# Second matrix sum of a Fourier feed-forward layer for even and odd rows apart, with another order of vector and GpSimd work around it

## The chip, the cores and the metric

One Trainium2 chip; the kernel runs on one of its cores. The metric is device time in microseconds of one launch. The core's engines each run their own instruction stream in order and wait for one another by semaphores: TensorE (PE in the profile; PEld is its weight loads), VectorE (DVE), ScalarE (ACT), GpSimd (POOL) and SyncE (SP), which here only issues transfers. Matmuls write to PSUM, all else lives in SBUF. All data are float32.

## What is computed

A cross-attention block and a Fourier feed-forward layer, both with a residual:

```python
x = x + xattn(layernorm(x), ctx, mask, wq, bq, wk, bk, wv, bv, wo, bo)   # 16 heads of 32
x = x + ffn(layernorm(x), w_freq_real, w_freq_imag, bias)

# ffn:
w = complex(w_freq_real, w_freq_imag)          # 512 x 512
y = real(ifft(fft(x) @ w)) + bias
```

x is 2 x 2048 x 512, the context 2 x 128 x 512. In attention a score is multiplied by the mask, and a score of exactly 0 becomes -1e9 before the softmax over 128 keys.

The feed-forward layer is linear in its input, so it equals a product with one real 512 x 512 matrix. The kernel computes this matrix once (`m_ffn`), by two sums with tables of cosines and sines, and then multiplies every row by it.

## The kernel before

**Work and order.** The 4096 query rows are cut in 8 groups of 512, and each group in 4 tiles of 128. A tile is named (i, t), group and place in it; (1, 0), (1, 1) and (1, 2) are the fifth to seventh. The schedule is written out by hand: each engine runs its instructions in the order of the program's text, and the tile framework adds only the waits for data and for buffers.

For a tile, `begin` (L764) issues the scores on PE (`scores`, L316) into two PSUM banks, one for each half of the heads. For each half, `masked` (L343) multiplies by the mask on DVE (L345, reading PSUM), `maxima` (L349) marks zeros and finds minima on DVE (L352, L354, L355), `exponentials` (L357) does 8 exponentials with sums on ACT (L361), and `divided` (L370) a reciprocal on DVE (L373) and the division, normally on POOL (L374). Once both halves are divided, `transposed_weights` (L380) transposes the weights on PE (L400) and copies them out of PSUM on ACT (L391). `context` (L414) multiplies them with the values for a whole group. `Project` (o, L446) and `Ffn` (y, L489) are the products with `wo` and `m_ffn`; DVE adds the residual (L463, L528). `Queries` (q, L285) are the query products, `relative` (L234), `query_statistics` (L261), `query_norm` (L274) and `query_transposes` (L278) the layer norm in front of them; `relative` runs on POOL (L244) or ACT (L241, L242). `output_bias` (L438) adds a bias on POOL (L442). From tile (1, 2) on, `slot` (L769) holds the order of a tile; what it shall finish in the next tile is put on the list `carried`.

**Buffers.** PSUM has two buffers each for scores (`ps_sc`), transposes (`ps_tp`) and products (`ps_mm`). Work tiles rotate over a few buffers by tag: 2 for "parts" and "sums", 4 for "rel", 5 for the weights "w".

**The matrix.** `First` (L647) makes the first sum, four blocks of 128 rows, `half`. Its cosine and sine sums are each split by even and odd table rows, so that only the first quarter of the columns (QD = 128) is computed: eight matmuls of 127 to 129 columns for a block, two for each of four stretches of the bank (L672). `evict` copies the bank out on ACT (L685), `first` makes sums and differences of even and odd rows on POOL (L693, L695), and `second` sums and differences of the cosine and sine part on DVE (L706, L707), writing the second half of the columns backwards.

`Mirrored` (L727) makes the second sum, four blocks of `m_ffn`, m[0] to m[3]. It is split into cosines (even) and sines (odd) only: four matmuls of 257 or 255 columns for a block (L738). ACT evicts the even part with a bias `add` and the odd part (L748, L754), and POOL forms low = even + odd and, mirrored, high = even - odd (L755, L756). `add` comes from four rows of `half` through transfers (`load_first_rows`, L712) and one small transpose (`first_rows`, L719).

The blocks m[0] to m[2] stand in the hand-written order of tile (1, 0) (L985 to L1010), m[3] in that of tile (1, 1) (L1012 to L1032). The first y that needs them is that of `slot(1, 3)`.

Of the kernel before, what the change touches and what calls it, by code (L numbers as in the profile page):

```python
# [9 lines left out]
FP = mybir.dt.float32  # L10
# [12 lines left out]
def kernel(  # L23
# [261 lines left out]
    class Queries:  # L285


        def __init__(self, i, g, first=0, spare=False):
            self.i, self.g, self.first, self.spare = i, g, first, spare
# [13 lines left out]
        def evict(self, eng=nc.scalar):  # L303
            dst = qTs[self.i][:, self.g, self.first * P :]
            bias = bq[:, self.g : self.g + 1]
            if eng is nc.scalar:
                nc.scalar.activation(dst, self.ps, AF.Identity, bias=bias)
            else:
                eng.tensor_scalar(dst, self.ps, bias, None, ALU.add)
# [70 lines left out]
    def transposed_weights(i, t, first, end, eng=None, banks=None, later=None):  # L380

        if t == 0 and first == 0:
            pts[i] = [big_tile("pt", 6, f"pt_{i}_{g}") for g in range(NC)]
        ws = weights[i, t]

        def copy(g, ps):
            dst = pts[i][g][:, :, t * P : (t + 1) * P]
            if eng:
                eng.tensor_copy(dst, ps)
            else:  # L390
                nc.scalar.copy(dst, ps)  # L391

        for g in range(first, end):
            ps = (
                banks[g]
                if banks
                else ps_tp.tile([P, NR, P], FP, tag="tp", name=f"tpw_{i}_{t}_{g}")
            )
            for r in range(NR):
                nc.tensor.transpose(  # L400
                    ps[:, r, :], ws[r // 2].w[:, (r % 2) * NC + g, :], ident
                )
            if later is not None:
                later.append((copy, g, ps))
            elif not banks:
                copy(g, ps)
        if banks and later is None:
            for g in range(first, end):
                copy(g, banks[g])
# [234 lines left out]

    QD = HD // 2

    class First:  # L647


# [9 lines left out]
        def pe(self, between=()):  # L659
            ps = self.ps = ps_mm.tile([P, D], FP, tag="mm", name=self.name)  # L660
            at = 0


            for k, table, odd, n in (
                (0, cosines, 0, QD + 1),
                (0, cosines, 1, QD),
                (1, sines, 0, QD - 1),
                (1, sines, 1, QD),
            ):
                for b in range(2):  # L670
                    c = b * HC + odd
                    nc.tensor.matmul(  # L672
                        ps[:, at : at + n],
                        self.lhs[k](c),
                        table[:, c, :n],
                        start=(b == 0),
                        stop=(b == 1),
                    )
                at += n
                if at == D // 2 + 1:  # L680
                    call(between)
# [17 lines left out]
                    op,  # L699
                )  # L700

        def second(self):
            u = self.u
            cos, sin = u[:, :, 0, : QD - 1], u[:, :, 1, : QD - 1]
            d = self.dst.rearrange("p (a n) -> p a n", a=2)
            nc.vector.tensor_tensor(d[:, :, 1:QD], cos, sin, ALU.add)  # L706
            nc.vector.tensor_tensor(d[:, ::-1, HD - 1 : QD : -1], cos, sin, ALU.subtract)  # L707

    def half_of(g):
        return lambda i: half[:, i, g * P : (g + 1) * P]  # L710
# [13 lines left out]
        nc.scalar.copy(add, ps)  # L724
        return add

    class Mirrored:  # L727

        def __init__(self, name, lhs, dst):
            self.name, self.lhs, self.dst = name, lhs, dst

        def pe(self):
            ps = ps_mm.tile([P, D], FP, tag="mm", name=self.name)
            self.even, self.odd = ps[:, : HD + 1], ps[:, HD + 1 :]
            for i in range(NC):
                nc.tensor.matmul(  # L738
                    self.even if i < HC else self.odd,
                    self.lhs(i),  # L740
                    cosines[:, HC + i, :] if i < HC else sines[:, i, :],
                    start=(i % HC == 0),
                    stop=(i % HC == HC - 1),
                )

        def evict(self, add, eng=nc.gpsimd):
            low, high = self.dst[:, 1:HD], self.dst[:, D - 1 : HD : -1]
            nc.scalar.activation(  # L748
                self.dst[:, : HD + 1], self.even, AF.Identity, bias=add
            )  # L750
            odd = self.odd
            if eng is nc.gpsimd:
                odd = work.tile([P, HD - 1], FP, tag="odd", name=f"odd_{self.name}")
                nc.scalar.copy(odd, self.odd)  # L754
            eng.tensor_tensor(high, low, odd, ALU.subtract)  # L755
            eng.tensor_tensor(low, low, odd, ALU.add)  # L756

    carried = []

# [116 lines left out]


    h = [First(what, g) for what in range(2) for g in range(HC)]
    m = [Mirrored(f"m_{g}", half_of(g), m_ffn[:, g, :]) for g in range(NC)]
    rest = [Queries(0, g, 1, g >= HC) for g in range(NC)]  # L880
    q = [Queries(1, g) for g in range(NC)]
    values = [Values(b) for b in range(B)]
# [96 lines left out]
    w[1].exponentials()  # L979
    run(q[0])  # L980
    transposed_weights(0, 2, HC, NC)
    w[1].divided()

    load_mask(2)
    w = begin(1, 0)  # L985
    w[0].masked()
    m[0].pe()
    add = first_rows("add_m", rows_m)
    m[0].evict(add[:, 0:1])
    relative(3, 0, nc.scalar)  # L990
    w[0].maxima()
    relative(3, 1, nc.gpsimd)
    m[1].pe()
    m[1].evict(add[:, 1:2])
    relative(3, 2, nc.gpsimd)
    transposed_weights(0, 3, 0, HC)
    relative(3, 3, nc.scalar)
    w[0].exponentials()
    w[1].masked()
    w[1].maxima()  # L1000
    w[0].divided()
    m[2].pe()
    m[2].evict(add[:, 2:3])
    transposed_weights(0, 3, HC, NC)
    w[1].exponentials()
    query_statistics(3, 0, 2)
    q[1].pe()
    q[1].evict(nc.vector)
    w[1].divided()
    query_statistics(3, 2, TG)  # L1010

    w = begin(1, 1)  # L1012
    w[0].masked()
    context(0, 0, NC, nc.scalar, True)
    m[3].pe()
    m[3].evict(add[:, 3:4])
    w[0].maxima()
    q[2].pe()
    w[0].exponentials()
# [9 lines left out]
    query_norm(3, 0)  # L1029
    query_norm(3, 1)  # L1030
    w[0].divided()
    carried.append(lambda half=w[1]: half.divided(nc.vector))  # L1032


    for i in range(1, last - 1):
        p, pp, n, nn = i - 1, i - 2, i + 1, i + 2
        q = [Queries(n, g) for g in range(NC)]
        q_nn = Queries(nn, 0)
        o = [Project(p, t) for t in range(TG)]
        f_p = Ffn(p, 0)  # L1040
        if i > 1:
            load_rows(nn)
            load_mask(n)
            load_residual(p)
            f_pp = [Ffn(pp, t) for t in range(TG)]
            slot(
                i,
                0,
                [f_pp[1], f_pp[2], q[1]],
                turned=(p, TG - 1),  # L1050
                early=[(ffn_transposes, pp, 2)],
                pool=[(relative, nn, t, nc.gpsimd) for t in range(TG)],
                on_b=[(ffn_norm, pp, 3), (query_statistics, nn, 0, 2)],
                on_c=[(query_statistics, nn, 2, TG)],
            )
            slot(
                i,
                1,
                [q[2], q[3], f_pp[3]],
                turned=(i, 0),  # L1060
                early=[(context, p, 0, NC, nc.scalar, True), (ffn_transposes, pp, 3)],
                pool=[(output_bias, p)],
                on_b=[(query_norm, nn, 0), (query_norm, nn, 1)],
            )
        slot(
            i,
            2,
            o[:3],
            turned=(i, 1),
            early=[(query_transposes, nn, 0), (query_transposes, nn, 1)],  # L1070
            pool=[(output_bias, p, 0, HC)] if i == 1 else [],
            mid_a=[(output_bias, p, HC, TG)] if i == 1 else [],
            on_a=[(ffn_statistics, p, 0)],
            on_m=[(ffn_norm, p, 0), (query_norm, nn, 2), (query_norm, nn, 3)],
            on_c=[(ffn_statistics, p, 1)],
            end=[(ffn_transposes, p, 0)],
        )
        slot(
            i,
            3,  # L1080
            [o[3], f_p, q_nn],
            turned=(i, 2),
            early=[(query_transposes, nn, 2), (query_transposes, nn, 3)],
            on_a=[(ffn_statistics, p, 2)],
            on_b=[(ffn_norm, p, 1), (ffn_statistics, p, 3)],
            on_c=[(ffn_norm, p, 2)],
            end=[(ffn_transposes, p, 1)],
        )
# [201 lines left out]
```

## Time and profile before

| | us |
|---|---|
| median of 3 runs (lowest, highest) | 528.55 (528.09, 528.93) |
| profiled execution, time | 528.42 |
| profiled execution, span | 526.2 |

Busy time in stretches of the span, in us; the granted TensorE clock is 1.00 in all of them:

| stretch (us) | what | PE | DVE | ACT | POOL |
|---|---|---|---|---|---|
| 0 to 75.70 | set-up, first sum, group 0 | 73.93 | 59.33 | 47.94 | 47.93 |
| 75.70 to 125.13 | second sum, tiles (1, 0) to (1, 3), up to the first y | 48.57 | 41.98 | 37.27 | 35.00 |
| 125.13 to 442.30 | steady state | 317.06 | 273.69 | 222.39 | 203.63 |
| 442.30 to 526.20 | last tiles and their products | 80.40 | 54.83 | 35.62 | 43.36 |

How to read the profile: a float32 matmul shows as two records, so "x8" is four matmuls. Matmuls are pipelined and their ends are modelled, so the distance from one start to the next tells more of PE than a duration. A timeline line has start, duration, engine, line of the kernel, operation, names and shapes, a count, and, in brackets, the engine's idle time before it with what ended it. The chain of waits is followed back from the last instruction: at each step to what released it, or to the instruction before it on its engine.

### The profile page before, as it was taken

What the parts mean: (1) busy time and instruction counts of PE and PEld (TensorE: products, weight loads), DVE (VectorE), ACT (ScalarE), POOL (GpSimd) and SP (SyncE); (2) the same over time, 40 slices, a digit from 0 to 9 for tenths busy, and PEclk for the clock granted to TensorE, in tenths of its full rate; (3) what the DMA queues carried; (4) which work ended last, traced back from release to release, by engine and by line L of the source; (5) the groups of instructions that cost most, each with busy time, mean ns of one, the idle gap of its engine ahead of it and who ended that gap; (6) DMA issues with size and microseconds to landing.
All of it is one profiled execution on the core that took longest, in us unless ns stands there. A gap on an engine that the chain in (4) does not pass through costs nothing.

```text
span 526.2 us, 8813 instructions
## 1 busy us (share of the span) xinstructions
PE 520.0 (99%) x3028; PEld 295.1 (56%) x3028; DVE 429.8 (82%) x613; ACT 343.2 (65%) x1300; POOL 329.9 (63%) x272
## 2 busy tenths in 40 slices
PE   8999999999999999999999999999999999999997
PEld 7756676655545555555545555455545555455444
DVE  4789897799997988889887988889876899998351
ACT  3367789776666777766667777666686677666210
POOL 3779368566993569635993559634764466756450
PEclk9999999999999999999999999999999999999999
DMA  8962030000600042000600024000312001301002
GB/s 320 382 239 80 1 102 1 0 2 0 222 21 21 1 140 101 1 21 1 220 21 14 7 85 156 1 22 0 121 42 72 29 12 50 102 1 61 20 0 81
DMA packets 22892, 36.49 MB, mean 69 GB/s; under 512 B 2104, under 2 KB 7488, under 8 KB 22848
## 3 DMA queue, kind: packets, MB, share of 16 engines
q1 hardware_dynamic: 22160, 34.75, 19.3%
q10 hardware_dynamic: 688, 1.18, 0.6%
q8 instruction: 24, 0.39, 0.3%
q14 instruction: 20, 0.16, 0.1%
HBM read 27.53 MB, written 8.39 MB: 68 GB/s over the span
## 4 chain that ended last, share of the span: by engine, by line
PE 84%; DVE 8%; ACT 6%; issue 1%; POOL 0%; ACTq 0%; POOLq 0%; DVEq 0%
PE y L210 18%; PE q L210 18%; PE o L210 16%; PE tpw L400 8%; PE sc L326 6%; ACT w L361 5%; PE c L426 4%; PE tp_a L194 3%; PE tp_f L194 3%; DVE w L352 2%; DVE nmax L354 2%; PE half L672 1%; PE k L572 1%; PE v L210 1%; DVE w L345 1%; ACT pt L391 1%
## 5 line engine op out<-in xcount | busy, mean ns | idle before, releaser
L361 ACT ACTIVATE w<-w,nmax 128x128 f32<-128x128 f32 x512 | 198.3, 395 | 18.3 <-DVE nmax L355 14.6
L374 POOL TENSOR_TENSOR w<-w,rden 128x1024 f32<-128x1024 f32 x61 | 116.1, 1908 | 73.6 <-DVE rden L373 57.0
L210 PE MATMUL o<-wo,cT 128*128 128x512 f32 x256 | 115.4, 594 | 0.1
L210 PE MATMUL y<-m_ffn,nT 128*128 128x512 f32 x248 | 112.5, 595 | 0.3 <-DVE nT L198 0.2
L210 PE MATMUL q<-xnT,wq 128*128 128x512 f32 (+1 forms) x256 | 111.6, 580 | 0.0
L391 ACT COPY pt<-tpw 128x512 f32<-128x512 f32 x120 | 64.0, 586 | 54.8 <-PE tpw L400 54.7
L361 ACT ACTIVATION_READ_ACCUMULATOR w<-w,nmax 128x1 f32 x512 | 99.3, 194 | 0.0
L352 DVE SCALAR_TENSOR_TENSOR w<-w 128x1024 f32<-128x1024 f32 x64 | 88.3, 1380 | 0.9
L345 DVE TENSOR_TENSOR w<-sc,mask 128x1024 f32<-128x1024 f32 x64 | 77.5, 1212 | 10.1 <-PE sc L326 9.4
L354 DVE TENSOR_REDUCE nmax<-w 128x8 f32<-128x1024 f32 x64 | 78.1, 1220 | 2.2
L400 PEld LDWEIGHTS tpw<-ident,w 128*128 128x128 f32 x496 | 57.7, 141 | 30.5 <-issue 28.4
L210 PEld LDWEIGHTS o<-wo,cT 128*128 128x128 f32 x256 | 46.2, 190 | 47.8 <-issue 46.2
L210 PEld LDWEIGHTS q<-xnT,wq 128*128 128x128 f32 x256 | 46.4, 190 | 44.6 <-issue 40.2
L210 PEld LDWEIGHTS y<-m_ffn,nT 128*128 128x128 f32 x248 | 44.5, 190 | 45.2 <-issue 43.5
L482 POOL TENSOR_TENSOR x<-x,bf 128x512 f32<-128x512 f32 x32 | 50.4, 1574 | 24.7 <-DVE norm_f L227 24.7
L400 PE MATMUL tpw<-ident,w 128*128 128x128 f32 x496 | 64.3, 273 | 0.0
L223 POOL TENSOR_SCALAR rstd_f<-mv_f 128x1 f32<-128x1 f32 x32 | 19.0, 594 | 61.1 <-DVE mv_f L220 61.1
L442 POOL TENSOR_TENSOR x<-x,bo 128x512 f32<-128x512 f32 x32 | 47.3, 1509 | 0.0
L373 DVE RECIPROCAL rden<-den 128x8 f32<-128x8 f32 x64 | 12.7, 199 | 41.6 <-ACT w L361 41.4
L326 PEld LDWEIGHTS sc<-kT,qT 32*128 32x128 f32 x1024 | 31.5, 186 | 14.2 <-issue 12.5
L244 POOL TENSOR_SCALAR rel<-rows 128x512 f32<-128x512 f32 x23 | 38.5, 1688 | 1.2 <-DMA rows<-in_x_dram 1.2
L196 ACT COPY nT<-tp_f 128x512 f32<-128x512 f32 x29 | 16.9, 581 | 33.7 <-PE tp_f L194 33.5
(92 smaller groups left out, 551.5 us busy)
## 6 DMA issues: line engine op xcount, KB each, us to landing
rows<-in_x_dram SPq DMA_DIRECT2D x32, 256.0 KB, 4.2
x<-in_x_dram SPq DMA_DIRECT2D x32, 256.0 KB, 5.2
out_dram<-x SPq DMA_DIRECT2D x31, 256.0 KB, 2.0
mask<-in_mask_Bx1xSxS_fk_dram SPq DMA_DIRECT2D x8, 256.0 KB, 4.6
wk<-in_L_xattn_wk_w_dram ACTq DMA_DIRECT2D x2, 512.0 KB, 6.5
wq<-in_L_xattn_wq_w_dram SPq DMA_DIRECT2D x1, 1024.0 KB, 7.0
wr<-n_L_ffn_w_freq_real_dram SPq DMA_DIRECT2D x2, 512.0 KB
wi<-n_L_ffn_w_freq_imag_dram SPq DMA_DIRECT2D x2, 512.0 KB, 8.9
```

The lines of the kernel that those rows point to most:

```text
L210: nc.tensor.matmul(ps, lhs(c), rhs(c), start=(c == 0), stop=(c == NC - 1))
L244: eng.tensor_scalar(d, xt, xt[:, 0:1], None, ALU.subtract)
L326: nc.tensor.matmul(sc[r // 2][:, r % 2, g, :], qTs[i][rows, g, t * P : (t + 1) * P], kT[rows, g, b * K : (b + 1) * K], start=True, stop=True,)
L345: nc.vector.tensor_tensor(self.w, self.sc.rearrange("p r g k -> p (r g) k"), self.mrow, ALU.mult)
L352: nc.vector.scalar_tensor_tensor(w, w, 0.0, w, ALU.is_equal, ALU.subtract)
L354: nc.vector.tensor_reduce(self.nmax, w, AX.X, ALU.min)
L361: nc.scalar.activation(w[:, h, :], w[:, h, :], AF.Exp, bias=self.nmax[:, h : h + 1], scale=-UNIT, accum_out=self.den[:, h : h + 1],)
L374: eng.tensor_tensor(w, w, rden.unsqueeze(2).to_broadcast([P, HH, K]), ALU.mult)
L391: nc.scalar.copy(dst, ps)
L400: nc.tensor.transpose(ps[:, r, :], ws[r // 2].w[:, (r % 2) * NC + g, :], ident)
L442: nc.gpsimd.tensor_tensor(xs[:, t, :], xs[:, t, :], bo, ALU.add)
L482: nc.gpsimd.tensor_tensor(xt, xt, bf, ALU.add)
```

## The change

The list of (table half, table, odd, columns) of the first sum becomes a common `products`. The second sum gets the form of the first: `Second` takes the place of `Mirrored`. A block is four matmuls of 127 to 129 columns, each into its own stretch of the bank and each complete in itself; ACT evicts the bank in two instructions (129 columns with the bias, the rest without) into a work tile; then `first` on POOL and `second`, on DVE for m[0] and m[1], on POOL for m[2] and m[3], as its new argument `eng` says.

The order of tiles (1, 0) to (1, 2) changes too. m[1] is issued just behind m[0], and q[1] ahead of m[2]. `relative(3, 0)` moves ahead of the tile, and `relative(3, 3)` goes from ACT to POOL. The second division of tile (1, 0) and half of the statistics move behind the scores and the first masking of tile (1, 1). The second division of tile (1, 1) goes from DVE to POOL, with the first `output_bias` of group 0 ahead of it.

```diff
+    products = (
+        (0, cosines, 0, QD + 1),
+        (0, cosines, 1, QD),
+        (1, sines, 0, QD - 1),
+        (1, sines, 1, QD),
+    )
...
-        def second(self):
+        def second(self, eng=nc.vector):
...
-            nc.vector.tensor_tensor(d[:, :, 1:QD], cos, sin, ALU.add)
-            nc.vector.tensor_tensor(d[:, ::-1, HD - 1 : QD : -1], cos, sin, ALU.subtract)
+            eng.tensor_tensor(d[:, :, 1:QD], cos, sin, ALU.add)
+            eng.tensor_tensor(d[:, ::-1, HD - 1 : QD : -1], cos, sin, ALU.subtract)
...
-    class Mirrored:
+    class Second(First):
+        def __init__(self, g):
+            self.name = f"m_{g}"
+            self.dst = m_ffn[:, g, :]
+            self.lhs = half_of(g)
         def pe(self):
+            ps = self.ps = ps_mm.tile([P, D], FP, tag="mm", name=self.name)
+            at = 0
+            for k, table, odd, n in products:
                 nc.tensor.matmul(
+                    ps[:, at : at + n],
+                    self.lhs(k * HC + odd),
+                    table[:, HC + odd, :n],
+                    start=True,
+                    stop=True,
                 )
+                at += n
+        def evict(self, add):
+            t = self.t = work.tile([P, D], FP, tag="parts", name=f"t_{self.name}")
+            n = QD + 1
+            nc.scalar.activation(t[:, :n], self.ps[:, :n], AF.Identity, bias=add)
+            nc.scalar.copy(t[:, n:], self.ps[:, n:])
...
     transposed_weights(0, 2, HC, NC)
+    relative(3, 0, nc.scalar)
     w[1].divided()
     load_mask(2)
     w = begin(1, 0)
     w[0].masked()
     m[0].pe()
+    m[1].pe()
     add = first_rows("add_m", rows_m)
     m[0].evict(add[:, 0:1])
-    relative(3, 0, nc.scalar)
     w[0].maxima()
     relative(3, 1, nc.gpsimd)
-    m[1].pe()
-    m[1].evict(add[:, 1:2])
+    m[0].first()
     relative(3, 2, nc.gpsimd)
     transposed_weights(0, 3, 0, HC)
-    relative(3, 3, nc.scalar)
+    m[1].evict(add[:, 1:2])
+    m[1].first()
+    q[1].pe()
     w[0].exponentials()
     w[1].masked()
     w[1].maxima()
+    q[1].evict(nc.vector)
+    m[2].pe()
     w[0].divided()
-    m[2].pe()
+    relative(3, 3, nc.gpsimd)
+    transposed_weights(0, 3, HC, NC)
+    m[0].second()
+    m[1].second()
     m[2].evict(add[:, 2:3])
-    transposed_weights(0, 3, HC, NC)
+    m[2].first()
     w[1].exponentials()
     query_statistics(3, 0, 2)
-    q[1].pe()
-    q[1].evict(nc.vector)
-    w[1].divided()
-    query_statistics(3, 2, TG)
-
+    old = w
     w = begin(1, 1)
     w[0].masked()
+    old[1].divided()
+    query_statistics(3, 2, TG)
     context(0, 0, NC, nc.scalar, True)
     m[3].pe()
     m[3].evict(add[:, 3:4])
+    m[2].second(nc.gpsimd)
+    m[3].first()
+    m[3].second(nc.gpsimd)
     w[0].maxima()
...
     w[0].divided()
-    carried.append(lambda half=w[1]: half.divided(nc.vector))
+    output_bias(0, 0, 1)
+    carried.append(w[1].divided)
...
-            pool=[(output_bias, p, 0, HC)] if i == 1 else [],
+            pool=[(output_bias, p, 1, HC)] if i == 1 else [],
```

## The prediction

> **What bounds the kernel now.** I read the page first, then the chain of waits, then the timelines of the four engines from 75 to 126 us, the stretch that the change touches. The page says which engine matters:
>
> ```profile
> PE 520.0 (99%) x3028; PEld 295.1 (56%) x3028; DVE 429.8 (82%) x613; ACT 343.2 (65%) x1300; POOL 329.9 (63%) x272
> ```
>
> PE is busy all the time (and its granted clock is 1.00 in every stretch that I asked for), so a PE microsecond taken away ought to be a microsecond won. The chain of waits, followed back from the end, contradicts this for just our stretch (start, length, what):
>
> ```profile
> 79.06 1.94 PE m L738 x8
> ...
> 81.02 0.48 ACT m_ffn L748
> ...
> 96.80 0.18 DVE nmax L355
> ...
> 119.64 0.48 ACT nT L196
> 120.12 0.04 issue
> 120.16 0.66 PE tp_a L194 x4
> ```
>
> From 81 to 120 us the chain runs through ACT and DVE (evictions, exponentials, maxima), and PE comes back on it at 120.16. PE was packed full too, but its only idle time there is 0.73 us before that transpose and about 0.3 after. So two chains run side by side, about 1 us apart. From 125 to 441 us PE's pieces follow one another without a gap: what the first product of the second matrix (y, 125.13 us) gains or loses, the end gains or loses. I therefore forecast the start of that y.
>
> **The saved PE work.** The second sum's matmuls and the cheaper form already used in the first sum:
>
> ```profile
> 67.46 1.10 PE L672 MATMUL half<-dft,wi 128*128 128x129 f32 x8
> ...
> 76.74 2.00 PE L738 MATMUL m<-dft,half 128*128 128x257 f32 x8
> ...
> 120.16 0.66 PE L194 MATMUL tp_a<-ident,rel 128*128 128x128 f32 x4 [0.73 <-ACT nT L196]
> ```
>
> The durations (second column) include the pipeline's tail; from start to start the chain gives 1.93 for eight old records (one m) and 0.94 for eight of 128 columns (67.46 to 68.41). The new m has eight such records: 4 x (1.93 - 0.94) = 3.96 us less PE. Had the weight loads (190 ns each) set the pace, an m would take 1.5 us, but the first sum's eight records already go at 0.94.
>
> **What it adds.** Per m: ACT still evicts 512 columns in two instructions (0.62 us before; a single 512-column eviction of the first sum took 0.58, so 0.58 to 0.65, and ACT has idle time for either). POOL had two of 0.73; now `first` has 0.67 + 0.20 + 0.67 + 0.20 by the first sum's rows (L693, L695), 1.60 from start to start. `second` is two more of 254 columns: on DVE for m0 and m1, 0.33 each, 4 x 0.33 = 1.32 us; on POOL for m2 and m3. No POOL row has exactly that form; L693 (0.67) and the mirrored L755 (0.73) bound it from both sides. I take both; these end 1.2 us before POOL is wanted, so nothing follows. Moved: `relative(3,0)` goes into ACT's idle time at 77.6 (ACT waits there until 79.09), `relative(3,3)` goes from ACT to POOL (1.55), the division of tile 6's second half from DVE (1.38) to POOL (1.87), and one bias addition (1.25) ahead of that division on POOL. The DMA orders do not change; the four rows for `add` still land just before 78.86, so the first eviction cannot start before 79.29.
>
> **The price that the sum of busy times hides.** DVE and POOL exclude one another for some instructions:
>
> ```profile
> 74.59 2.10 POOL L374 TENSOR_TENSOR w<-w,rden 128x1024 f32<-128x1024 f32 x1
> ```
>
> ```profile
> 74.51 0.42 DVE L706 TENSOR_TENSOR half<-u_half 128x254 f32<-128x254 f32 x1 [0.73 <-POOL u_half L693]
> 74.85 2.12 DVE L707 TENSOR_TENSOR half<-u_half 128x254 f32<-128x254 f32 x1
> ...
> 107.35 2.28 DVE L352 SCALAR_TENSOR_TENSOR w<-w 128x1024 f32<-128x1024 f32 x1
> ...
> 139.33 0.54 DVE L355 TENSOR_SCALAR nmax<-nmax 128x8 f32<-128x8 f32 x1
> ```
>
> L707 is the second half of `second`: 0.41 alone, 2.12 when POOL's division got in between. L352 (1.22 alone) and even the tiny L355 (0.17) stretch likewise beside POOL's additions, and POOL's instructions stretch when DVE was first (L223, 0.23, took 1.11 at 113.86). Reads of PSUM (L345, L463), the reduction L354 and the statistics L219 never stretch. So who asks first holds until done. The change puts four more such instructions on DVE and fourteen more on POOL (16 of `first` and 4 of `second` for the 8 of before, one `relative`, one division) in the same stretch.
>
> One POOL instruction is milder. Beside L244 (`relative`, 1.57 us, from 139.16) the L355 above got through 0.53 us after L244's start, well before L244's end, so I let L244 block for 0.53. The Trainium skill, "SBUF — State Buffer", section "Who interferes with whom", says otherwise: whichever of the two engines issues first keeps the shared ports for the whole instruction. By that page the sum would end 1.6 us later, near 531.9 (an estimate); I take the row.
>
> **The sum.** I laid the instructions of all four engines end to end in the new order, with these durations, each starting when its engine is free and its inputs are ready (0.04 us after DVE or ACT, 0.07 after POOL, 0.2 after PE), first come first served between DVE and POOL. The old order laid the same way puts PE's q at 94.62 (trace 94.34), the scores of tile 7 at 103.25 (103.05), its weight transposes at 108.71 (108.52), and y at 125.50 (125.13). So the method is 0.1 to 0.4 late.
>
> DVE, from the first maxima of tile 5 (81.58 in the trace) to the first of tile 6 (96.97), took 15.39 us, of which 1.19 and 2.26 idle. In the new order the idle 3.45 goes, since no division waits at the head of the queue any more; `second` adds 1.32; 0.73 is waiting for m1's `first`, which stands on POOL behind two `relative`s; and waits behind POOL add 0.30 (L352), 0.11, 0.20, 0.10 and 1.90 (`second`; the last one behind the division of tile 5, as at 74.85), 0.55 (L352 behind the next division) and 0.64 (L355 behind m3's `first`), together 3.80. 15.39 - 3.45 + 1.32 + 0.73 + 3.80 = 17.79: maxima at 99.4 instead of 97.0.
>
> ACT follows: exponentials of tile 6 at 99.4 and 105.0 instead of 97.0 and 102.6, ending at 108.2. The scores of tile 7 wait for ACT's copies out of the borrowed bank until 103.6. The second half's division: reciprocal at 108.2; POOL is in the bias addition until 108.5; DVE's L352, asking at 108.3, goes next until 109.7; the division runs to 111.58. PE's transposes of those weights start at 111.65 instead of 108.52. From there PE is packed: 15.5 us to y, where the trace has 16.6, because the idle 1.0 at 119 to 121 is gone. y at 127.16.
>
> As a check by PE alone: 3.96 saved, idle 7.0 in place of 1.0 to 1.1 (largest: 2.47 before those transposes, 2.28 before the scores, 0.73, 0.50, 0.34): +2.0. Against my own laying of the old order it is +1.65, against the trace +2.03; I take **+1.8**. The profiled execution has a span of 526.2 and a time of 528.42, 0.13 below the median of 528.55. 528.42 + 1.8 = 530.2, and from the median 530.35: forecast **530.3**, slower.
>
> **Rivals.** *The ports cost little: faster.* If DVE's and POOL's instructions miss each other, the 3.8 us and the waits at 108 vanish. Then the maxima of tile 6 come at 94.9, the last exponentials end at 103.5, POOL divides to 105.9, PE transposes at 106.1, 2.4 sooner than 108.52, and the idle 1.0 goes as well: y 3.5 sooner, 525.0. For it: PE's saving is real, and the two DVE idles are filled. Against it: L707's 2.12, in the same pairing. It wins over the old kernel when the waits that I count (3.8 + 0.7 on DVE, 1.1 at the division) come to less than some 3.5 us.
>
> *One turn won: no change.* The single dearest wait is m1's last instruction behind tile 5's division. If `second` gets its turns, it saves 1.4 us: y at 125.7, 529.0. Which of the two asks first hangs on less than 0.4 us, so this is near.
>
> *The saving does not show on PE.* Were an m 1.5 us instead of 0.94, PE would come 2.3 later to places where it waits anyway (4 us in all up to 104): still about 530.3. So the matmuls hardly decide.
>
> **Chances.** Forecast, 529.6 to 531.8: 0.55. Slower still: 0.05. No change, within 0.2% (527.5 to 529.6, about what a measurement of this kernel can tell): 0.17. Faster: 0.23. The range leaves out the slowest 0.05 and, of the faster case, what goes beyond 526.0 (some 0.1): 526.0 to 531.8. The forecast's own range is 529.6 to 531.8.
>
> **What would show it.** Right: m rows of about 0.94 us per eight; PE idle before the transposes of tile 6's weights (2 us or more) and the scores of tile 7; a `second` on DVE of about 2.3 us beside POOL's division; the first maxima of tile 6 after 98.5. Wrong: `second` at 0.42 four times, the maxima of tile 6 before 96, y before 124. If the y starts late but the end does not, a later stretch had slack that the chain does not show.

## The result and the profile after

The changed kernel took 528.66 us (median of 12 runs, 528.33 to 529.56), the kernel before 528.41 beside it (12 runs, 528.09 to 529.26). The ratio is 1.0004, with a 95% interval of 0.9995 to 1.0013: no change that can be measured. The forecast was 530.3. The profiled execution has a span of 526.7 us. (The profile of the experiment e5 is of a disturbed execution and is not read; e11 is the same kernel again.)

The page's busy line first:

```profile
PE 518.3 (98%) x3028; PEld 293.8 (56%) x3028; DVE 432.2 (82%) x616; ACT 342.2 (65%) x1298; POOL 339.2 (64%) x286
```

PE is down by only 1.7 us and POOL up by 9.3. PE's timeline, where the brackets give the idle time before the line and what ended it:

```profile
77.21 2.05 PE L740 MATMUL m<-dft,half 128*128 128x129 f32 x16
...
84.03 1.05 PE L740 MATMUL m<-dft,half 128*128 128x129 f32 x8
...
90.85 1.16 PE L740 MATMUL m<-dft,half 128*128 128x129 f32 x8 [0.22 <-ACT cT L434]
92.31 3.70 PE L210 MATMUL q<-xnT,wq 128*128 128x512 f32 x8 [0.29 <-ACT cT L434]
...
102.63 1.16 PE L326 MATMUL sc<-kT,qT 32*128 32x128 f32 x28 [1.02 <-ACT pt L391]
...
110.34 0.88 PE L400 MATMUL tpw<-ident,w 128*128 128x128 f32 x6 [1.54 <-POOL w L374]
```

The second sum is as cheap as forecast: where PE does not wait inside a block, its eight records take 0.89 to 0.99 us from start to start. But idle time has opened at exactly the two places that the prediction named, before the scores of tile 7 and before the weight transposes of tile 6, and two smaller ones beside the copies of `context`. The old idle 0.73 at 120 us is gone. DVE's timeline at `second` and at the second division of tile 6:

```profile
86.77 0.39 DVE L707 TENSOR_TENSOR m_ffn<-u_m 128x254 f32<-128x254 f32 x1
87.08 0.41 DVE L708 TENSOR_TENSOR m_ffn<-u_m 128x254 f32<-128x254 f32 x1
88.06 0.43 DVE L707 TENSOR_TENSOR m_ffn<-u_m 128x254 f32<-128x254 f32 x1 [0.57 <-POOL u_m L694]
88.40 2.12 DVE L708 TENSOR_TENSOR m_ffn<-u_m 128x254 f32<-128x254 f32 x1
...
107.23 0.20 DVE L373 RECIPROCAL rden<-den 128x8 f32<-128x8 f32 x1 [2.29 <-ACT w L361]
107.35 1.18 DVE L352 SCALAR_TENSOR_TENSOR w<-w 128x1024 f32<-128x1024 f32 x1
```

and POOL's at the same two places:

```profile
88.14 2.10 POOL L374 TENSOR_TENSOR w<-w,rden 128x1024 f32<-128x1024 f32 x1
...
105.86 1.27 POOL L442 TENSOR_TENSOR x<-x,bo 128x512 f32<-128x512 f32 x1
107.58 2.70 POOL L374 TENSOR_TENSOR w<-w,rden 128x1024 f32<-128x1024 f32 x1 [0.46 <-DVE rden L373]
```

The last instruction of m1's `second` (88.40) takes 2.12 us in place of 0.41, because POOL's division began 0.26 us before it. At 107.58 it is the other way round: DVE's L352 has begun at 107.35, and the division takes 2.70 instead of 1.90. The chain of waits (start, length, what) runs through both places:

```profile
88.06 0.43 DVE m_ffn L707
88.49 2.03 DVE m_ffn L708
...
97.77 0.65 DVE nmax L355
...
107.58 2.71 POOL w L374
110.29 0.05 issue
110.34 0.88 PE tpw L400 x6
...
125.83 3.44 PE y L210 x8
```

It leaves PE at 79.4 and comes back at 110.34; in the kernel before it came back at 120.16.

**How places are compared.** From the first y to the end of the span every kernel below (e5 apart) takes 401.1 to 401.5 us, so y decides, as the prediction has it. But the set-up ahead differs from one execution to another: the scores of tile 5 begin between 75.59 and 76.72. The table therefore counts from those scores (first start in the timeline). "Maxima" is the end of the first half's maxima of tile 6, "division" the end of tile 6's second division. The time is the median less that of the kernel before on the same chip.

| kernel | maxima | division | y | y against before | time against before | ratio (95%) |
|---|---|---|---|---|---|---|
| before | 21.34 | 31.79 | 49.32 | | | |
| changed | 22.30 | 34.17 | 49.56 | +0.24 | +0.25 | 1.0004 (0.9995 to 1.0013) |
| e1 | 20.61 | 31.36 | 48.89 | -0.43 | +0.11 | 1.0008 (0.9996 to 1.0020) |
| e2 | 22.91 | 34.79 | 50.17 | +0.85 | +1.07 | 1.0020 (1.0011 to 1.0029) |
| e3 | 19.75 | 33.64 | 51.99 | (clock, see e3) | -0.35 | 1.0002 (0.9987 to 1.0016) |
| e4 | 19.57 | 33.48 | 48.86 | -0.46 | +0.04 | 1.0003 (0.9995 to 1.0012) |
| e5 | | | | | -1.90 | 0.9970 (0.9957 to 0.9982) |
| e6 | 21.16 | 31.74 | 48.21 | -1.11 | -1.05 | 0.9984 (0.9975 to 0.9993) |
| e7 | 20.97 | 32.84 | 48.23 | -1.09 | -0.85 | one run |
| e8 | 22.30 | 33.33 | 50.87 | +1.55 | +2.52 | 1.0041 (1.0029 to 1.0053) |
| e9 | 21.79 | 33.67 | 49.05 | -0.27 | -0.64 | 0.9991 (0.9982 to 1.0000) |
| e10 | 21.16 | 33.04 | 48.43 | -0.89 | -0.58 | 0.9990 (0.9981 to 0.9999) |
| e11 | 20.08 | 31.96 | 47.34 | -1.98 | -2.04 | 0.9965 (0.9952 to 0.9977) |

One profiled execution stands beside a median here, so a few tenths between the two columns mean nothing.

**Where the saved time went.** Taken from start to start on PE between the scores of tile 5 and y, the four blocks of the second sum take 3.8 us, where packed old blocks (in e6, in which PE never idles there) take 7.4. That is about 3.5 us less work. What PE waits in the same stretch, every step against the same step in a packed stretch, grew from 1.1 to 4.7 us: 1.8 at the weight transposes of tile 6, 1.5 at the scores of tile 7, 0.8 beside the copies of `context`, and 0.6 in two small places. The gain turned into new waits, almost one for one. (The bracketed idle times are smaller, since the modelled end of a matmul covers part of a gap.)

### The profile page after: what moved, and what is told of

Read it like the earlier page. It is cut to its first block, busy times and chain, and to the rows that moved or that the text cites. A ratio compares the mean times of both kernels' runs of the same rounds, so it can differ in the third digit from the quotient of the medians.

```text
span 526.7 us, 8840 instructions
## 1 busy us (share of the span) xinstructions
PE 518.3 (98%) x3028; PEld 293.8 (56%) x3028; DVE 432.2 (82%) x616; ACT 342.2 (65%) x1298; POOL 339.2 (64%) x286
## 4 chain that ended last, share of the span: by engine, by line
PE 86%; DVE 7%; ACT 4%; POOL 2%; issue 1%; ACTq 0%; POOLq 0%; DVEq 0%
PE y L210 18%; PE q L210 18%; PE o L210 18%; PE tpw L400 9%; PE sc L326 6%; PE c L426 4%; ACT w L361 3%; PE tp_a L194 3%; PE tp_f L194 3%; DVE w L352 2%; PE half L673 1%; DVE nmax L354 1%; PE k L572 1%; PE v L210 1%; DVE w L345 1%; PE busy L544 1%
## 5 line engine op out<-in xcount | busy, mean ns | idle before, releaser
L374 POOL TENSOR_TENSOR w<-w,rden 128x1024 f32<-128x1024 f32 x62 | 119.0, 1923 | 69.0 <-DVE rden L373 53.5
L352 DVE SCALAR_TENSOR_TENSOR w<-w 128x1024 f32<-128x1024 f32 x64 | 88.4, 1381 | 0.8
L442 POOL TENSOR_TENSOR x<-x,bo 128x512 f32<-128x512 f32 x32 | 45.4, 1449 | 0.0
L244 POOL TENSOR_SCALAR rel<-rows 128x512 f32<-128x512 f32 x24 | 41.2, 1729 | 1.5 <-PE tp_a L194 1.5
L326 PE MATMUL sc<-kT,qT 32*128 32x128 f32 x1024 | 38.0, 283 | 1.0 <-ACT pt L391 1.0
```

The source lines that it names most:

```text
L244: eng.tensor_scalar(d, xt, xt[:, 0:1], None, ALU.subtract)
L326: nc.tensor.matmul(sc[r // 2][:, r % 2, g, :], qTs[i][rows, g, t * P : (t + 1) * P], kT[rows, g, b * K : (b + 1) * K], start=True, stop=True,)
L352: nc.vector.scalar_tensor_tensor(w, w, 0.0, w, ALU.is_equal, ALU.subtract)
L374: eng.tensor_tensor(w, w, rden.unsqueeze(2).to_broadcast([P, HH, K]), ALU.mult)
L442: nc.gpsimd.tensor_tensor(xs[:, t, :], xs[:, t, :], bo, ALU.add)
```

## The experiments

The theories, as the expectations name them. **A**, that of the prediction: PE's saved time is eaten by DVE's waits for GpSimd, and what queues behind them. **B**: the new order costs, and the form of the sum by itself gains 1 to 4 us. **C**: neither matters much; GpSimd's longer queue ahead of tile 6's second division decides. **D** was formed after e1 to e4: the order of tile 5 (two `relative`s ahead of `first`, q[1]'s eviction ahead of `second`) costs some 0.9 us, the rest of the new order gains, and y is set by the DVE and ACT chain and not by PE.

**e1: the new form in the old order.** `first` and `second` stand behind the evictions where the old blocks had their work. Against the kernel before, without the classes:

```diff
     m[0].evict(add[:, 0:1])
+    m[0].first()
     relative(3, 0, nc.scalar)
...
     m[1].evict(add[:, 1:2])
+    m[1].first()
     relative(3, 2, nc.gpsimd)
...
     transposed_weights(0, 3, HC, NC)
+    m[0].second()
+    m[1].second()
+    m[2].first()
...
     m[3].evict(add[:, 3:4])
+    m[2].second(nc.gpsimd)
+    m[3].first()
+    m[3].second(nc.gpsimd)
```

> The new form of the second sum (four quarter-column matmuls, first on GpSimd, second on DVE for blocks 0 and 1) in the order of the kernel before. Theory A (the saved PE time is real and is eaten by DVE's waits for GpSimd, and by what queues behind them): PE's rows for a block fall from 1.93 to about 0.95 us, yet the first maxima of tile 6 come at 98.5 to 99.5 us (97.0 before) and the time is 1.3 to 2.3 us above before. Theory B (the new order is what costs, the form by itself gains): 1 to 4 us below before. Rival C (GpSimd's longer queue alone): about 1 us above, with the maxima of tile 6 not later than 97.5.

No change in time. `second` on DVE, the division and the L352 behind it:

```profile
86.12 0.38 DVE L707 TENSOR_TENSOR m_ffn<-u_m 128x254 f32<-128x254 f32 x1
86.42 0.82 DVE L708 TENSOR_TENSOR m_ffn<-u_m 128x254 f32<-128x254 f32 x1
87.17 0.41 DVE L707 TENSOR_TENSOR m_ffn<-u_m 128x254 f32<-128x254 f32 x1
87.50 0.41 DVE L708 TENSOR_TENSOR m_ffn<-u_m 128x254 f32<-128x254 f32 x1
...
105.81 1.67 DVE L374 TENSOR_TENSOR w<-w,rden 128x1024 f32<-128x1024 f32 x1
107.41 2.28 DVE L352 SCALAR_TENSOR_TENSOR w<-w 128x1024 f32<-128x1024 f32 x1
```

With `first` early on POOL, `second` waits only 0.4 us for POOL, and the maxima of tile 6 come 0.7 sooner than before instead of later. So A's form in the expectation falls: `second` as such costs little; it cost much in the changed kernel because of where it stood. B's gain did not come either. DVE's division and L352 are held up by the four bias additions on POOL:

```profile
103.90 6.92 POOL L442 TENSOR_TENSOR x<-x,bo 128x512 f32<-128x512 f32 x4
```

**e2: the old form in the new order.** `Mirrored` as before, without `first` and `second`, in the changed order. Against the changed kernel:

```diff
-    class Second(First):
+    class Mirrored:
...
-    m[0].first()
...
-    m[1].first()
...
-    m[0].second()
-    m[1].second()
...
-    m[2].first()
...
-    m[2].second(nc.gpsimd)
-    m[3].first()
-    m[3].second(nc.gpsimd)
```

> The old form (257 and 255 columns, combined on GpSimd) in the new order. Theory A: no instruction of the second sum stands on DVE, but PE's 4 us are back, and the division of tile 6's second half on GpSimd still comes late: 0.5 to 1.5 us above before. Theory B (the order costs): 3 us or more above before. Rival C (GpSimd's queue decides): GpSimd has some 6 us less to do here than in the changed kernel, so the transposes of tile 6's weights come at 108.5 or sooner and the time is within 0.5 us of before.

1.07 us slower than before. The order costs without any `second` on DVE. The changed kernel is 0.8 us faster than this (+0.25 against +1.07), so the form does gain under the new order.

**e3 and e4: m0's and m1's `second` later.** e3 moves the two behind the first division of tile 6, with four buffers for the sums instead of two, so that they no longer meet the division of tile 5. e4 takes e3 and also the early bias addition away again.

```diff
-            u = self.u = work.tile([P, 2, 2, QD], FP, tag="sums", name=f"u_{self.name}")
+            u = self.u = work.tile([P, 2, 2, QD], FP, tag="sums", bufs=4, name=f"u_{self.name}")
...
-    m[0].second()
-    m[1].second()
...
     w[0].divided()
+    m[0].second()
+    m[1].second()
     output_bias(0, 0, 1)
```

and for e4 also

```diff
-    output_bias(0, 0, 1)
...
-            pool=[(output_bias, p, 1, HC)] if i == 1 else [],
+            pool=[(output_bias, p, 0, HC)] if i == 1 else [],
```

> The changed kernel with the two DVE seconds moved behind the norms of tile 6 (and four buffers for the sums, so that GpSimd does not wait for them). Theory A in its pure form: the maxima of tile 6 come 2.5 to 3.5 us sooner than in the changed kernel (about 95.5 instead of 98.4) and so does the end: 2.5 to 3 us below the changed kernel. Rival C (GpSimd's queue ahead of the division of tile 6's second half decides): the maxima come sooner just the same, but the division does not, and the time is 0.3 to 0.8 us below the changed kernel. Laying the rows end to end gives 0.6.

> As the run before, and the first bias addition (1.25 us on GpSimd) back behind the division of tile 6's second half. Theory A: as the run before, no further gain, since DVE's maxima are not touched. Rival C: another 1.0 to 1.3 us, some 1.8 us below the changed kernel and 1 to 1.5 us below before (0.2 to 0.3%).

The maxima of tile 6 come 2.5 to 2.7 us sooner, as they should if the turn behind the division cost 1.7 and the `second`s the rest. Yet by the ratios neither is apart from the changed kernel. e3 is 0.6 us below it by the medians, inside the intervals; that is what C and the laid rows had, and not the 2.5 to 3 of A. e4's further gain, which C needed, did not come. In e4 the late `second` met the next division, first on DVE

```profile
102.07 0.94 DVE L707 TENSOR_TENSOR m_ffn<-u_m 128x254 f32<-128x254 f32 x1
102.94 2.11 DVE L708 TENSOR_TENSOR m_ffn<-u_m 128x254 f32<-128x254 f32 x1
```

and on POOL

```profile
102.70 2.08 POOL L374 TENSOR_TENSOR w<-w,rden 128x1024 f32<-128x1024 f32 x1
```

So the same price, 2.11 for 0.41, is paid after all, only further down. It holds up DVE's next reciprocal until 106.11, and tile 6's second division ends only 0.7 us sooner (33.48 against 34.17). C is weakened: with the bias addition gone from POOL's queue nothing moved.

In e3's profiled execution PE's idle time before those transposes had a price of its own. The windows of 5 us, with the granted clock third from the right:

```profile
100.00:105.00 5.00, 5.00 (x48) 2.98 (x47) 5.00 (x8) 5.00 (x21) 5.00 (x7) 1.00 0.00 0
105.00:110.00 5.00, 2.41 (x8) 0.93 (x6) 4.93 (x6) 1.61 (x4) 4.75 (x3) 0.95 0.00 0
110.00:115.00 5.00, 4.76 (x11) 2.70 (x12) 4.90 (x7) 3.77 (x16) 5.00 (x5) 0.50 0.02 3
115.00:120.00 5.00, 5.00 (x18) 2.69 (x17) 4.36 (x7) 2.50 (x11) 3.15 (x4) 0.87 0.00 2
120.00:125.00 5.00, 5.00 (x51) 3.31 (x50) 2.55 (x5) 3.74 (x15) 3.28 (x4) 1.00 0.00 0
```

That execution took 531.74 us and is not the rule: the median of the 12 is 527.88.

**e5 and e11: the form in the old order of tile 5, with the rest of the new order.** e1, and `relative(3, 0)` early, the second division of tile 6 on POOL and the bias addition ahead of its first division.

```diff
     transposed_weights(0, 2, HC, NC)
+    relative(3, 0, nc.scalar)
     w[1].divided()
...
     m[0].first()
-    relative(3, 0, nc.scalar)
     w[0].maxima()
...
+    output_bias(0, 0, 1)
     w[0].divided()
-    carried.append(lambda half=w[1]: half.divided(nc.vector))
+    carried.append(w[1].divided)
...
-            pool=[(output_bias, p, 0, HC)] if i == 1 else [],
+            pool=[(output_bias, p, 1, HC)] if i == 1 else [],
```

> The new form in the order of the kernel before, with three pieces of the new order: relative(3,0) ahead of tile 5, the second division of tile 6 on GpSimd, one bias addition ahead of it (here also ahead of the first division, where GpSimd stood idle for 2 us). Theory D, formed from the first four runs (the new order of tile 5, with relatives and q[1]'s eviction ahead of first and second, costs about 0.9 us and the rest of the new order gains): y comes 1.2 to 2 us sooner than before, counted from the scores of tile 5 (49.3 before), and the time is 1.2 to 2 us below before (0.3%). Theory A (the saving goes to waits between DVE and GpSimd, whatever the order): no more than the 0.4 us of the form alone.

> The kernel of e5_form_part_order once more, for its profile: y 47.6 to 47.9 us after the scores of tile 5 (49.3 before), the maxima of tile 6 at 20.1 to 20.4 (21.3), tile 6's second division done by 32.2; 526.3 to 526.7 us.

526.40 and 526.31 us, 1.9 and 2.0 below before: this version beats both kernels, as D said. DVE in e11:

```profile
85.59 0.38 DVE L707 TENSOR_TENSOR m_ffn<-u_m 128x254 f32<-128x254 f32 x1
85.89 0.82 DVE L708 TENSOR_TENSOR m_ffn<-u_m 128x254 f32<-128x254 f32 x1
86.63 0.41 DVE L707 TENSOR_TENSOR m_ffn<-u_m 128x254 f32<-128x254 f32 x1
86.97 0.41 DVE L708 TENSOR_TENSOR m_ffn<-u_m 128x254 f32<-128x254 f32 x1
...
88.91 0.72 DVE L309 TENSOR_SCALAR qT<-q,bq 128x512 f32<-128x512 f32 x1
...
104.62 1.17 DVE L352 SCALAR_TENSOR_TENSOR w<-w 128x1024 f32<-128x1024 f32 x1
```

and POOL's last instruction ahead of the division of tile 5:

```profile
85.52 1.80 POOL L244 TENSOR_SCALAR rel<-rows 128x512 f32<-128x512 f32 x1
```

The last `second` has begun (86.97) before that division starts on POOL (87.29), and takes its own 0.41. The maxima of tile 6 come 2.22 us sooner than in the changed kernel, the division ends 2.21 sooner and y comes 2.22 sooner: one difference, made in tile 5, is carried unchanged to y. PE still waits for the division:

```profile
107.60 0.87 PE L400 MATMUL tpw<-ident,w 128*128 128x128 f32 x6 [1.21 <-POOL w L374]
```

**e6: only the bias additions of the kernel before earlier,** all four ahead of tile 6's first division.

```diff
+    output_bias(0)
     w[0].divided()
...
-            pool=[(output_bias, p, 0, HC)] if i == 1 else [],
-            mid_a=[(output_bias, p, HC, TG)] if i == 1 else [],
```

> The kernel before, old form and old order, only with the four bias additions of group 0 moved into GpSimd's idle time at 97 to 102 us, ahead of the first division of tile 6. Theory D and A both (what sets y is DVE's chain at tile 7, which stands behind GpSimd's additions for about 1.4 us, and not PE's matmuls): DVE's division falls from 1.38 to 1.2 us, the L352 behind it from 2.28 to 1.2, PE's idle 0.7 before the transpose goes, and y comes 0.7 to 1.0 us sooner, the time likewise. If PE's work sets y: no change.

1.05 us faster than before. DVE's division and L352, held up before, run at their own speed:

```profile
106.20 1.22 DVE L374 TENSOR_TENSOR w<-w,rden 128x1024 f32<-128x1024 f32 x1
107.34 1.22 DVE L352 SCALAR_TENSOR_TENSOR w<-w 128x1024 f32<-128x1024 f32 x1
```

since POOL is through with the additions:

```profile
96.73 5.95 POOL L442 TENSOR_TENSOR x<-x,bo 128x512 f32<-128x512 f32 x4
```

The 0.73 us of PE idle at 120 us was thus a consequence of POOL's additions beside DVE's division at 107, 13 us earlier. No PE idle is left in the stretch, from start to start; with the old form PE is then the bound.

**e10: the old form with e11's order.**

```diff
+    relative(3, 0, nc.scalar)
     w[1].divided()
...
     m[0].evict(add[:, 0:1])
-    relative(3, 0, nc.scalar)
...
+    output_bias(0, 0, 1)
     w[0].divided()
-    carried.append(lambda half=w[1]: half.divided(nc.vector))
+    carried.append(w[1].divided)
...
-            pool=[(output_bias, p, 0, HC)] if i == 1 else [],
+            pool=[(output_bias, p, 1, HC)] if i == 1 else [],
```

> The counterpart of the form in part of the new order, but with the old form: relative(3,0) early, tile 6's second division on GpSimd, one bias addition ahead. Theory D: PE's work counts only where DVE's and ACT's chain is out of the way; here PE and that chain are close to one another, y comes 0.3 to 0.5 us sooner than before, and the new form is worth 1.0 to 1.3 us against this kernel. If the form is worth nothing in any order: as fast as the form in part of the new order (526.4).

0.58 us faster than before, 1.46 slower than e11. So in this order the form is worth 1.5 us (1.1 by y) of the 3.5 that PE saves, and the three moves together 0.6. From start to start PE waits 0.2 us in e10 and 2.7 in e11: here the form gains until the DVE and ACT chain becomes the bound.

**e7: the turn at the division taken away.** The changed kernel, but the first division of tile 5 on POOL is a memset: half of that tile's weights are a constant, 0.01. The memset only writes.

```diff
+            if eng is None:
+                nc.gpsimd.memset(w, 0.01)
+                return
...
-    w[0].divided()
+    w[0].divided(None)
```

> The changed kernel with the division of tile 5's first half replaced by a GpSimd memset of the same 128 x 1024 weights (the first half of tile 5's weights is a constant here). It only writes. If the exclusion comes from GpSimd's reading: m1's second instruction on DVE, 2.12 us beside the division, takes 0.4 us although the memset runs beside it. If any GpSimd instruction holds DVE up: it lasts until the memset ends, 1 us or more.

DVE (this kernel has three lines more, so L711 is L708 of the others):

```profile
88.10 0.42 DVE L710 TENSOR_TENSOR m_ffn<-u_m 128x254 f32<-128x254 f32 x1 [0.57 <-POOL u_m L697]
88.44 0.42 DVE L711 TENSOR_TENSOR m_ffn<-u_m 128x254 f32<-128x254 f32 x1
```

POOL:

```profile
88.16 0.95 POOL L375 MEMSET w<- 128x1024 f32 x1
```

The last `second` ran wholly inside the memset and took 0.42 instead of 2.12. So DVE is not held up by POOL being busy as such; what the memset lacks is the reading. The maxima come 1.33 us sooner and so does y; 0.95 us of POOL's own time went too, so this bounds the price of that turn rather than giving it alone.

The Trainium skill, "SBUF — State Buffer", section "Who interferes with whom", says just this of a VectorE instruction with two SBUF inputs: it contends with a GpSimd instruction that reads SBUF, not with one that only writes. The 0.42 agrees.

**e8: tile 6's second division back on DVE,** in the changed kernel.

```diff
-    output_bias(0, 0, 1)
-    carried.append(w[1].divided)
+    carried.append(lambda half=w[1]: half.divided(nc.vector))
```

> The changed kernel with the second division of tile 6 back on DVE and the bias addition back behind it. Rival C (GpSimd's queue sets y): the transposes of tile 6's weights come 1 us or more sooner (34.2 us after the scores of tile 5 in the changed kernel) and y as well. Theory D: the transposes come 0.6 to 1.2 us sooner, but DVE's chain of tile 7 starts behind the division and behind the additions, so y comes 0.3 to 1.1 us later, and the time is 0.3 to 1.1 us above the changed kernel.

2.5 us slower than before, more than expected. The division does end sooner (33.33 against 34.17), but it meets POOL's additions, and the L352 behind it too:

```profile
107.03 1.96 DVE L374 TENSOR_TENSOR w<-w,rden 128x1024 f32<-128x1024 f32 x1
108.91 2.29 DVE L352 SCALAR_TENSOR_TENSOR w<-w 128x1024 f32<-128x1024 f32 x1
```

```profile
105.40 6.91 POOL L442 TENSOR_TENSOR x<-x,bo 128x512 f32<-128x512 f32 x4
```

As in the kernel before, DVE's lateness comes back on PE at 121 us (idle 0.92). So the move of the division to POOL, with the early bias addition that belongs to it, is a part of the change that gains; by C it should have been the part that costs. The median rose by 1.0 us more than y, but the profiled execution took 529.77 us, against a median of 530.82, and its span is 1.6 us longer than before, as its y says. No trace of an execution near the median is kept.

**e9: the changed kernel with m0's and m1's `first` ahead of the `relative`s on POOL.**

```diff
-    relative(3, 1, nc.gpsimd)
     m[0].first()
-    relative(3, 2, nc.gpsimd)
+    relative(3, 1, nc.gpsimd)
...
     m[1].first()
+    relative(3, 2, nc.gpsimd)
```

> The changed kernel with only GpSimd's order in tile 5 altered: m[0].first ahead of relative(3,1), and m[1].first ahead of relative(3,2). Theory D: m1's second on DVE no longer waits for GpSimd (idle 0.57 us before it in the changed kernel), the maxima of tile 6 come 0.7 to 1.0 us sooner (22.3 us after the scores of tile 5) and y and the time 0.6 to 1.0 us sooner than in the changed kernel. Theory A with any order alike: no change.

y comes 0.5 us sooner than in the changed kernel, and the time is 0.9 lower (-0.64 against +0.25). The wait of DVE for m1's `first` (0.57) is what this takes away; the maxima come 0.51 sooner, less than the 0.7 to 1.0 expected. The turn behind the division stays:

```profile
86.77 0.74 DVE L309 TENSOR_SCALAR qT<-q,bq 128x512 f32<-128x512 f32 x1
...
88.50 2.11 DVE L708 TENSOR_TENSOR m_ffn<-u_m 128x254 f32<-128x254 f32 x1
```

Here L309, q[1]'s eviction, stands ahead of the four `second`s; in e11 it stands behind them. Counted from the scores of tile 5, the division starts at 11.62 in e9 and 11.70 in e11, and the first `second` at 10.82 and 10.00. So the division comes at the same place, and most of the 0.8 us by which `second` is later in e9 is that eviction; no run moves it alone. The rest of the way to e11's maxima, 1.71 us, is the 1.70 that this turn costs.

## Why the prediction was right in its range and wrong in its number

**The range.** 528.66 lies in the stated range, 526.0 to 531.8, but only because the range takes in the rivals. The forecast's own part of it, 529.6 to 531.8, misses, and so does "slower"; what came is the case "no change", which had 0.17. That the range holds is its width, and not the sum.

**Right.** The form: m takes 0.89 to 0.99 per block, so the rival that PE does not show the saving is out. The place of the new waits on PE. The dearest turn: `second` behind the division of tile 5, 2.12. The order at tile 6's second half: DVE's L352 goes first, and the division waits. From the transposes to y 15.5 us (110.34 to 125.83), as laid. And that the idle at 119 to 121 us goes. Of its own signs, the maxima after 98.5 us and the idle of 2 us or more came out just short (98.41, in an execution whose set-up ran 0.5 us late; 1.8 from start to start).

**Wrong is a size: the waits behind POOL.** From the first maxima of tile 5 to those of tile 6 the sum had 17.79 us; it took 16.38. In the sum's terms (forecast, then measured):

| term | forecast | measured |
|---|---|---|
| L352, tile 5 | 0.30 | 0.13 |
| L355, tile 5 | none | 0.16 |
| `second` of m0, two | 0.11, 0.20 | 0, 0 |
| waiting for m1's `first` | 0.73 | 0.57 |
| `second` of m1, two | 0.10, 1.90 | 0, 1.71 |
| L352, tile 6 | 0.55 | 0.42 |
| L355, tile 6 | 0.64 | 0.47 |
| together | 4.53 | 3.46 |

Nearly every term is too large by 0.1 to 0.2. The two waits of m0's `second` did not come at all: DVE went first there. For the others, the laying let a waiting DVE instruction begin when POOL's had ended in the profile, and some hundredths later. The trace has it otherwise: the L708 that waited ended at 90.52, so with its own 0.41 it began at 90.11, while POOL's division shows until 90.24. The wait ends some 0.13 us before the profile's end of the POOL instruction. The row at 74.85 that the prediction shows had this already: 2.12 for 0.41 is a wait of 1.71, not 1.90. By the table, the four waits that came as forecast are 0.66 too large together, of which 4 x 0.13 = 0.52 is that end; three that did not come had 0.41; the wait for `first` is 0.16 too large, and L355 of tile 5, put at nothing, takes 0.16 back. The other 0.3 us are durations and latencies that each were some hundredths too long.

**And a turn that was not taken.** At tile 6's second half the sum had POOL in the bias addition until 108.5. That addition was over at 107.13, before the reciprocal at 107.23, so that the division waited only for DVE's L352, 0.8 us. It ended at 34.17 instead of 35.94 after tile 5's scores (111.58 less 75.64): 1.8 us less, of which 1.4 comes from the maxima. All of it is found again at y: 49.56 in place of 51.35 (127.16 less 75.64, and less 0.17, since the chain starts y that much later than the timeline).

**What that makes of the sum.** +2.03 was forecast for y against the trace, +0.24 was measured. The sum is a small difference of large terms, 3.96 saved against 6.0 more idle; the saving was 3.5 and the new waits 3.6. The saving was itself too large by 0.5, because the old blocks, one after the other in a packed stretch, take 1.74 to 1.94 and not 1.93 each.

**The rivals.** "One turn won" gave 529.0 and so stands nearest, but its mechanism did not happen: the turn was lost, as forecast, and the time stayed the same for another reason, the many small waits. What it says is still seen: where the turn is won without moving anything else (e7), y is 1.3 us sooner, near the 1.4 that the rival named, though e7 also takes 0.95 us off POOL. "The ports cost little: faster" needed waits of less than some 3.5 us, on DVE and at the division together; they were 3.46 and 0.8, so it missed its point by 0.8 us.

**What the prediction did not do** is part the form from the order. Against before, the form alone is worth nothing measurable (e1), the order alone costs 1.07 (e2). But the order is not one thing: early `relative(3, 0)`, the division on POOL and the early bias addition gain together (e10; for the last two e8, by its opposite), while the order of tile 5 loses the 2.2 us by which e11 is ahead at the maxima of tile 6: 0.5 by the `relative`s ahead of `first` (e9), and 1.7 because `second` comes so late that it meets the division. That q[1]'s eviction makes it so late is read from the traces of e9 and e11 and not tested alone. Theory D stands, with its cost larger than the 0.9 it named; A is right on the mechanism in the changed kernel, and wrong that the form must bring it.

**Open.** Why a wait ends before POOL's end in the profile (POOL's spans are rough). Why the median of e8 lies 1 us above its profiled execution. And why the set-up ahead of tile 5 varies by up to 1.1 us between executions; no part of the change is needed for it, since e10 and e11 are at 75.79 and 75.59 and e2 at 76.60.

## What to carry to other kernels

An engine that is busy 99% of the time need not be the bound. Here a chain through other engines ran within about 1 us of it, and the same saving of 3.5 us was worth nothing measurable (before to e1), 0.8 us (e2 to changed) or 1.5 us (e10 to e11), depending on what stood around it. Where VectorE and GpSimd share work, place small two-input VectorE instructions ahead of the long GpSimd instruction that they would meet; one that came 0.3 us too late here waited 1.7 us, nearly all that was left of it, and a move that avoids one meeting should be followed to the next. A forecast that is the difference of two large sums deserves a range of both signs, and the parts of a change deserve a sum each.

## What the runs showed of the hardware

A PE gap can cost more than itself. In e3's profiled execution the gap before tile 6's weight transposes,

```profile
110.24 1.54 PE L400 MATMUL tpw<-ident,w 128*128 128x128 f32 x6 [2.83 <-POOL w L374]
```

was followed by a granted clock of 0.50 in the next 5 us and 0.87 in the 5 after, and y came at 51.99 where e4, whose gap of 2.66 us left the clock at 1.00, has 48.86: 3.1 us later, 3.0 of them behind the division. Most runs do not show it: the mean granted clock is below 0.999 in three of e3's 12 runs (0.993, 0.997, 0.997; 531.74, 529.97 and 529.64 us) and in three of e4's 11 (0.996; 529.08 to 529.41 us, where the median is 528.27). The 1.54 us gap of the changed kernel left the clock at 1.00.

The Trainium skill, "TensorE: Matmul & The Clock Gate", section "What's actually happening", has the clock halved after an idle window of about 3.4 us, with windows that run free of the kernel. The level of 0.50, and that it comes in some executions only, agree; but a gap of 2.83 us, at most 3.21 from start to start, was enough here, and the measurement decides.

The exclusion between VectorE and GpSimd was gone where GpSimd only wrote (0.42 us beside a memset, e7, against 2.12 beside a division, which reads). In the changed kernel it is over about 0.13 us before the profile's end of the GpSimd instruction; the same 0.13 stands in the kernel before (74.59 and 74.85) and in e9.

`relative` on GpSimd (L244) holds VectorE up in its first part only. In e11 it runs from 85.52 to 87.32; the `second` at 85.89 takes 0.82, and the two behind it start inside L244 and take 0.41 each. That bears out the row from which the prediction let L244 block for 0.53 us, and not the block for the whole instruction, with 531.9, that it gave beside it.
